# Hats' last steps four slots later, a projection load on another queue, two more steps ahead of a resizing product

## The chip, the cores and the metric

The kernel runs on one core of one Trainium2 chip. The metric is the device time of one execution in microseconds (us). Before the change three runs took 9247.16, 9256.04 and 9267.85 us; the median is 9256.04 us.

A core has five instruction streams that wait for each other by semaphores: TensorE (PE, whose weight loads stand apart as PEld), VectorE (DVE), ScalarE (ACT), GpSimd (POOL) and SyncE (SP). Each runs its own instructions strictly in order. A DMA is issued by an instruction on SP, ACT or POOL; if that instruction has to wait, everything behind it on the same engine waits too. The profile numbers the DMA queues: q1 carries what SP issues, q10 what ACT issues, q0 what POOL issues.

## The reference, cut to what matters

The input is 32 images of 96 x 56 x 56 floats. Layer 0 is an inverted bottleneck: a 1x1 expansion to 576 channels, a depthwise 3x3, a squeeze gate, a 1x1 **projection** back to 96 channels and a residual sum. Layer 1 takes that sum `x` and does this:

```python
mag = jnp.abs(jnp.fft.rfft2(x, norm='ortho'))
fe = mag.mean(1, keepdims=True)                 # summed over channels, then resized to 56 x 56
...
y = x * ca * sa                                 # channel and spatial attention, both from mag and x
magy = jnp.abs(jnp.fft.rfft2(y, norm='ortho')).mean(1, keepdims=True)
freq_e = jax.image.resize(magy, (b, 1, h, w), method='bilinear')
aux = jnp.concatenate([y, coord, freq_e], 1)
offset = _conv(aux, off_w, off_b, (1, 1))       # 9 taps x 2 coordinates for each pixel
gate = jax.nn.sigmoid(_conv(jax.nn.relu(_conv(aux, dg1_w, dg1_b, (1, 1))), dg2_w, dg2_b))
y_base = _conv(y, base_w, base_b, (1, 1))
sampled = _grid_sample_taps(y, px, py)          # bilinear samples of y at pixel + offset
y_def = jnp.einsum('bcthw,oct->bohw', sampled, def_w.reshape(c, c, 9))
z = (1 - gate) * y_base + gate * y_def          # then a normalisation over all images, and relu(zn + x)
```

## The kernel before, in words

Three stages of three different images are worked on at once, and `layers` weaves their instructions together.

- **The bands** (image b). An image is cut into 7 bands of 8 rows. The samples of a band are made without a gather: for each tile of 4 x 4 pixels the bilinear weights over an 8 x 8 block of y are written as a matrix and multiplied with that block on PE (`sample_tiles`, L725), ACT copies the products to `v` (L729), `pack` (L736) copies the last taps of `v` to spare partitions, and `deform` (L744) multiplies `v` with the deformable weights. A band has two halves of 7 tiles.
- **second(b+1)**: `attend`, the projection of layer 0 and both attentions of the next image.
- **first(b+2)**: `hidden`, expansion and depthwise of the image after that.

`second` and `first` are Python generators. Each `yield` ends a step. The bands set the beat: each call of `pump` is a **slot**, a band has 17 of them (one after each of its 14 tiles, three at its end), so an image has 119. In each slot `pump` takes from each generator as many steps as are due, then runs what stands in the list `later` with a slot number that has been reached:

```python
streams[:] = [[second(b + 1), 0, n_second, slot + 3, slot + length - 8],
              [first(b + 2), 0, n_first, slot, slot + length]]
...
due = st[2] * min(1.0, (slot - st[3]) / (st[4] - st[3]))
```

Here `length` is 119 and the count starts at the image's sixth band (`turn` = 5). `n_second` is counted by running `second(0)` once; counting the yields gives 61, and 40 for `n_first`. So step k of `second` comes at slot x = floor(3 + 108 (k - 1) / 61) + 1 of its image, which is used below.

What the change touches:

- **Hats** (`offsets`, L648 to 679). While band n is sampled, the offsets of band n+2 are found: joint convolution (L606, with `hid` L626), offsets copied to `at` (L655) and written to DRAM as `od` (POOL's queue, L659); in the ninth step SP loads them back, repeated over partitions, as `ht` (L671, one buffer only). Six steps later ACT turns distances into hat weights, max(0, 1 - |d|), with two activations in place (L674, L675), and the next step writes them to DRAM as `hd` on ACT's queue (L678). The generator gets one step at the band's start and one after each of the 14 tiles, so the activations stand behind the last tile's copies, ahead of `pack`, and L678 behind `pack`. `weights_load` (SP, L689 and L690) reads `hd` half a band later into `wc` and `wr`, DVE multiplies them (L696), and the half after that uses them on PE.
- **The projection** (`project_loads` L300 to 307, `project` L315 to 337). The depthwise output lies in DRAM (`h2d`, written by ACT's queue, L224). The projection makes 7 rows of each image half at a time, q = 0 to 3. Its input comes in two tiles with one buffer each: `hq0` (units 0 to 3, the first image half) and `hq1` (units 4 to 8). Per q there are four steps: matmuls on `hq0` (L324); the load of `hq0` for q+1; matmuls on `hq1` (L324, L330), ACT's two copies (L334) and the load of `hq1` for q+1; the residual sum and store on POOL (L467, L468).
- **The resizing product** (`resized_spectrum`, L420 to 436). One step sums the magnitudes over channels on DVE (`m2`, named `m_fe` or `m_fy`, L428); the next multiplies the sum with the resizing matrix on PE (L431). It runs twice for each image.
- **The transforms' loads** (`dft_mag`, L362): after the projection the three first groups of `x` are loaded by SP from what POOL stored.

Who orders what: SP's instructions stay exactly in the order in which the program issues them (`manual_schedule`). The other engines' order is chosen by a scheduler when the program is built; `keep_in_program_order` pins one instruction behind everything issued earlier on its engine.

Of the kernel before, what the change touches and what calls it, by code (L numbers as in the profile page):

```python
# [7 lines left out]
FP = mybir.dt.float32  # L8
I32 = mybir.dt.int32
AF = mybir.ActivationFunctionType  # L10
# [23 lines left out]
EW = ER * W  # L34
NBD = H // RB
BW = NBW
TS = 4
NTX = W // TS
# [4 lines left out]
SB = TS + 2 * REACH  # L43
NS = SB * SB
KP = NTAP * TP
# [256 lines left out]
def project_loads(nc, p, h2d, q, half):  # L302

    u0, u1 = ((0, NCH - 1), (NCH - 1, len(UNITS)))[half]
    hq = p["hq"].tile([128, u1 - u0, EW], FP, name=f"hq{half}")
    nc.sync.dma_start(hq, h2d[u0:u1, :, q * EW : (q + 1) * EW].rearrange("u p n -> p u n"))
    return [(UNITS[u][0], hq[:, u - u0]) for u in range(u0, u1)]


# [112 lines left out]
def resized_spectrum(nc, p, mag, name, scale=None):  # L422


    m2 = p["sp"].tile([2 * WX, V], FP, name=f"m_{name}")
    if scale is not None:
        nc.vector.tensor_tensor(mag, mag, scale.unsqueeze(2).to_broadcast([2 * WX, NP, V]), ALU.mult)
    nc.vector.tensor_reduce(m2, mag.rearrange("p q u -> p u q"), AX.X, ALU.add)  # L428
    yield
    pf = p["acc"].tile([128, 512], FP, name="acc")  # L430
    nc.tensor.matmul(pf[:V, : 2 * W], m2, p["w"]["RT2"], start=True, stop=True)  # L431
    rs = p["sp"].tile([V, 2, W], FP, name=name)
    nc.scalar.copy(rs.rearrange("p m w -> p (m w)"), pf[:V, : 2 * W])
    p["resized"] = rs
    yield


def attend(tc, p, b, x, h2d, pooled, x1, given=False):
# [7 lines left out]
    if not given:  # L446
        NQ = HH // ER
        first = project_loads(nc, p, h2d, 0, 0)
        yield from squeeze(nc, p, pooled)
        rows = [first, project_loads(nc, p, h2d, 0, 1)]  # L450
        for _ in range(2):
            yield
        for q in range(NQ):
            at = q, q + NQ
            xrs = [residual_load(nc, p, x, k) for k in at]
            outs = project(nc, p, rows)
            next(outs)
            yield
            if q + 1 < NQ:
                first = project_loads(nc, p, h2d, q + 1, 0)  # L460
            yield
            os = next(outs)
            if q + 1 < NQ:
                rows = [first, project_loads(nc, p, h2d, q + 1, 1)]
            yield
            for k, o, xr in zip(at, os, xrs):
                nc.gpsimd.tensor_tensor(o, o, xr, ALU.add)  # L467
                nc.gpsimd.dma_start(x1[:, k * EW : (k + 1) * EW], o)  # L468
            yield
# [10 lines left out]
    nc.scalar.mul(s3[:, 0], pm[:H, :W], 1.0 / C)  # L480
    yield
    yield from resized_spectrum(nc, p, mag, "fe")
    fe = p["resized"]
    mas = p["sp"].tile([2 * WX, 2, NP], FP, name="mas")
# [82 lines left out]
    yield from dft_mag(nc, p, x1, sa)  # L567
    yield
    yield from resized_spectrum(nc, p, p["magnitude"], "fy", cx)
    fy = p["resized"]  # L570
    pz = p["acc"].tile([128, 512], FP, name="acc")
# [48 lines left out]
def joint_conv(nc, p, yp, j, hid):  # L620


    w = p["w"]
    pa = bank(p)
    conv3(nc, pa[:, :BW], w["joint"], yp, CJ, j)
    nc.scalar.activation(hid, pa[:DMID, :BW], AF.Relu, bias=w["dg1b"][:DMID])  # L626
    yb = p["yb"].tile([C, BW], FP, name="yb")
    yield yb, pa[OFF0 : OFF0 + NOFF, :BW]
    nc.scalar.activation(yb[BC:], pa[OFF0 + QC :, :BW], AF.Identity, bias=w["cv"]("base_b")[BC:])
    pb = bank(p)  # L630
    for k in range(NTAP):
        dy, dx = divmod(k, 3)
        r0 = j * RB + dy + PD - 1
        for i in range(2):
            nc.tensor.matmul(pb[i * BC : (i + 1) * BC, : BW // 2].rearrange("p (h w) -> p h w", h=RB // 2), w["base"][:, k],  # L635
                             yp[:C, r0 + i * RB // 2 : r0 + (i + 1) * RB // 2, dx + PD - 1 : dx + PD - 1 + W],
                             start=(k == 0), stop=(k == NTAP - 1))
    yield
    for i in range(2):
        nc.scalar.activation(yb[:BC, i * BW // 2 : (i + 1) * BW // 2], pb[i * BC : (i + 1) * BC, : BW // 2], AF.Identity,  # L640
                             bias=w["cv"]("base_b")[:BC])
    yield


def offsets(nc, p, yp, j, top, hid, ybs, hds):

    w = p["w"]
    joint = joint_conv(nc, p, yp, j, hid)  # L650
    yb, pa = next(joint)
    ybs.append(yb)
    at = p["off"].tile([NOFF, NTX, 2, TP], FP, name="at")
    for s in range(2):
        nc.vector.tensor_copy(at[:, :, s].rearrange("o t (r c) -> o t r c", r=TS),  # L655
                              pa[:, s * BW // 2 : (s + 1) * BW // 2].rearrange("o (r t c) -> o t r c", r=TS, t=NTX))
    yield
    od = p["dp"].tile([NTX, 2, NOFF, TP], FP, name="od")
    nc.gpsimd.dma_start(od.rearrange("t s o p -> o (t s) p"), at.rearrange("o t s p -> o (t s) p"))  # L659
    yield  # L660
    next(joint)
    yield
    next(joint)
    yield
    next(joint, None)
    nc.vector.tensor_reduce(top, at.rearrange("o t s p -> o (t s p)"), AX.X, ALU.max, apply_absolute_value=True)
    for _ in range(4):
        yield
    ht = p["ht"].tile([SB * NTX, 4, KP], FP, name="ht")
    src = od.rearrange("t s o p -> t (s o p)").unsqueeze(0).to_broadcast([SB, NTX, 4 * KP])  # L670
    nc.sync.dma_start(ht.rearrange("q n k -> q (n k)"), src)  # L671
    for _ in range(6):
        yield
    p["tc"].keep_in_program_order(nc.scalar.activation(ht, ht, AF.Abs, bias=w["blk"]))  # L674
    nc.scalar.activation(ht, ht, AF.Relu, bias=w["one"], scale=-1.0)  # L675
    yield
    hd = p["dp"].tile([4, SB, NTX, KP], FP, name="hd")
    nc.scalar.dma_start(hd.rearrange("x i t n -> (i t) x n"), ht)  # L678
    hds.append(hd)


def weights_load(nc, p, hd, h):
# [237 lines left out]
def padded(nc, p, a, images):  # L920

    cp = p["cp"]
    yps = [cp.tile([CJ, HY, WY], FP, name=f"yp{i}") for i in range(images)]
    for t in yps:
        nc.gpsimd.memset(t, 0.0)
        nc.sync.dma_start(t[C : C + 4, PD : PD + H, PD : PD + W], a["coord"])
        nc.sync.dma_start(t[CA:, PD : PD + H, PD : PD + W], a["place"])
    p["x2"], p["n_x2"] = [cp.tile([2 * H, CG, WX], FP, name=f"x2_{i}") for i in range(3)], 0
    for t in p["x2"]:
        nc.gpsimd.memset(t, 0.0)  # L930
    p["s4"] = [cp.tile([H, 3, WP], FP, name=f"s4_{i}") for i in range(2)]
    for t in p["s4"]:
        nc.gpsimd.memset(t, 0.0)
    return yps
# [8 lines left out]
def layers(tc, a, dp, x1d, zd, stats, far):  # L943
# [6 lines left out]
    nc = tc.nc  # L950
    B = x1d.shape[0]
    with ExitStack() as ctx:
        p = {"tc": tc, "dp": ctx.enter_context(tc.tile_pool(name="l1d", bufs=3, space=DRAM))}
# [3 lines left out]
        yp, = padded(nc, p, a, 1)  # L957
        top = p["cp"].tile([NOFF, NBD + 1], FP, name="top")
# [20 lines left out]
        streams, later = [], []  # L979
        slot = 0  # L980
# [96 lines left out]
        bands = [(b, j) for b in range(B) for j in range(NBD)]  # L1077
        hids, gates, ybs, hds, ready = [], [], [], [], []

        def find(n):  # L1080
            if n % 2 == 0:
                hids.append(p["hid"].tile([2 * NS, BW], FP, name="hid"))
            hid = hids[n // 2][n % 2 * NS : n % 2 * NS + DMID]
            return offsets(nc, p, yp, bands[n][1], top[:, n % NBD : n % NBD + 1], hid, ybs, hds)

        for n in range(2):
            for _ in beside(find(n)):
                pass
# [20 lines left out]
        for n, (b, j) in enumerate(bands):  # L1109
            if j == 0:  # L1110
                st = p["st"].tile([C, NBD, 6], FP, name="st")
            if j == turn:
                drain()
                refill(b + 1, 3 * RB)
                flush()
                start(b + 1, slots)
            more = find(n + 2) if n + 2 < len(bands) else iter(())
            next(more, None)
            for h in range(2):
# [385 lines left out]
```

## Time and profile before

| | |
|---|---|
| three runs, us | 9247.16, 9256.04, 9267.85 |
| the profiled execution, us | 9239.07, of which 9237.3 is the span |
| mean granted PE clock | 0.933 |
| busy PE / PEld / DVE / ACT / POOL | 89% / 56% / 78% / 58% / 27% |
| steady part, 700 to 8925 us | PE busy 7664.74 of 8225 us, DVE 6590.52, ACT 4998.23; PE clock 0.95; DMA engines 0.56 |
| start, 0 to 700 us | PE busy 539.88 us |
| end, 8925 to 9237 us (normalisation) | PE busy 17.22 us, DMA engines 0.91 |

How to read the views. "Busy" is the time in which an engine has an instruction under way. The view of waits names, for each engine, the instruction that sat idle, what ended the wait, the sum in us, how often, and the longest. The timeline lists instructions with their start and length; the bracket is the idle time before the first one and what ended it. The view of stretches gives, for a window of the span, the busy time of each engine, the granted PE clock (1.00 is full speed), the mean busy share of the 16 DMA engines and GB/s. A queue's name with q (SPq, ACTq) is the sequencer that waits and issues DMAs. In the steady part an image takes about 269 us, and the pattern of one image repeats in the next.

### The profile page before, as it was taken

The numbers are of one execution on the slowest core, as the hardware profiler recorded it, in microseconds if no ns is written. First come the engines' busy times: TensorE is split into PE (matmuls) and PEld (weight loads), VectorE is DVE, ScalarE is ACT, GpSimd is POOL, SyncE is SP. The second block draws the span as 40 slices with busy tenths as digits, with TensorE's granted clock in tenths as the row PEclk, the third lists the DMA queues.
The fourth block names the chain that finished last, engine by engine and source line by source line (L and its number), as shares of the span: only waits on it lengthen the run. The fifth ranks groups of instructions, "written<-read, shape, count | busy, mean of one in ns | idle before, by whom it ended". The sixth has DMA issues, their size and how long they took to land. (4 is left out here: it accounts for less than half of the span.)

```text
span 9237.3 us, 138081 instructions
## 1 busy us (share of the span) xinstructions
PE 8221.8 (89%) x52406; PEld 5208.4 (56%) x52406; DVE 7198.1 (78%) x6693; ACT 5369.4 (58%) x10486; POOL 2529.9 (27%) x2611
## 2 busy tenths in 40 slices
PE   5889999999999999899999999999999999999870
PEld 3455565565555556555555655555565655655550
DVE  7587788888888888887888888788888888887333
ACT  2355566666666566665566665566666655666553
POOL 0123233323223322332332223233222323322210
PEclk9889999999999999999999999999999999999985
DMA  2345555555555555555555555555555555554559
GB/s 88 95 137 156 165 166 159 165 150 150 161 163 163 163 164 149 150 157 165 163 157 160 148 153 157 164 167 159 159 152 153 160 166 163 160 160 140 131 181 417
DMA packets 1068764, 1486.54 MB, mean 161 GB/s; under 512 B 590190, under 2 KB 839838, under 8 KB 1055806
## 3 DMA queue, kind: packets, MB, share of 16 engines
q1 hardware_dynamic: 858995, 985.20, 39.2%
q10 hardware_dynamic: 153803, 329.80, 9.8%
q0 software_dynamic: 55296, 162.60, 6.8%
q8 instruction: 421, 6.90, 0.3%
q14 instruction: 249, 2.04, 0.1%
HBM read 1064.29 MB, written 412.65 MB: 160 GB/s over the span
## 5 line engine op out<-in xcount | busy, mean ns | idle before, releaser
L262 DVE SCALAR_TENSOR_TENSOR acch<-hp,w,acch 128x1512 f32<-128x1512 f32 (+1 forms) x2250 | 4397.3, 1954 | 38.2
L606 PE MATMUL mm<-yp,c_jointW 104*128 104x448 f32 x4032 | 1674.2, 567 | 27.7 <-ACT sq L414 19.2
L744 PE MATMUL pd<-v,c_def 128*96 128x224 f32 (+1 forms) x6272 | 1450.9, 378 | 225.2 <-ACT v L736 201.6
L707 POOL COPY ybl<-yp 96x448 f32<-96x448 f32 x896 | 1079.8, 1232 | 1698.5 <-PE mm L711 1697.5
L744 PEld LDWEIGHTS pd<-v,c_def 128*96 128x96 f32 (+1 forms) x6272 | 1046.2, 174 | 524.7 <-ACT v L736 229.2
L606 PEld LDWEIGHTS mm<-yp,c_jointW 104*128 104x128 f32 x4032 | 772.4, 196 | 808.1 <-issue 737.9
L725 PE MATMUL mm<-wc,yt 64*96 64x144 f32 x12544 | 1065.7, 298 | 56.8 <-ACT hp L173 38.0
L169 PE MATMUL mm<-xt,w 96*128 96x392 f32 (+3 forms) x2688 | 1061.2, 529 | 36.4 <-DMA xt<-in_x 33.0
L173 ACT ACTIVATE hp<-mm,sh,inv 128x392 f32<-128x392 f32 (+2 forms) x1216 | 813.2, 673 | 445.4 <-PE mm L169 400.6
L696 DVE TENSOR_TENSOR wc<-wc,wr 128x1008 f32<-128x1008 f32 x448 | 579.5, 1293 | 622.2 <-DMA wr<-hd 614.4
L729 ACT COPY v<-mm 96x288 f32<-96x288 f32 (+1 forms) x2688 | 1001.7, 443 | 100.3 <-PE mm L725 61.3
L725 PEld LDWEIGHTS mm<-wc,yt 64*96 64x96 f32 x12544 | 830.6, 162 | 358.5 <-issue 171.3
L324 PE MATMUL mm<-hq,w3s 128*96 128x392 f32 x2048 | 798.4, 537 | 157.2 <-DMA hq<-h2d 155.8
L635 PE MATMUL mm<-yp,c_base0W 96*64 96x224 f32 x8064 | 828.0, 357 | 0.0
L736 ACT COPY v<-v 32x448 f32<-32x448 f32 x1344 | 755.2, 562 | 29.9
L659 POOL DMA_DIRECT2D od<-at x224 | 186.0, 830 | 1947.6 <-DVE at L655 1386.0
L635 PEld LDWEIGHTS mm<-yp,c_base0W 96*64 96x64 f32 x8064 | 553.2, 135 | 276.2 <-issue 69.3
L713 ACT COPY yt<-mm 128x384 f32<-128x384 f32 (+1 forms) x896 | 350.1, 440 | 519.2 <-PE mm L711 514.5
L324 PEld LDWEIGHTS mm<-hq,w3s 128*96 128x96 f32 x2048 | 340.7, 175 | 513.6 <-issue 323.7
L222 ACT ACTIVATE acch<-acch,sh,inv 128x1568 f32<-128x1568 f32 x288 | 488.6, 1696 | 207.3 <-DVE acch L262 205.0
L626 ACT ACTIVATE hid<-mm,c_dg1b 50x448 f32<-50x448 f32 x224 | 140.7, 628 | 794.7 <-PE mm L606 784.6
L467 POOL TENSOR_TENSOR o<-o,xc 96x392 f32<-96x392 f32 x256 | 366.3, 1431 | 679.3 <-ACT o L334 677.8
(194 smaller groups left out, 9038.8 us busy)
## 6 DMA issues: line engine op xcount, KB each, us to landing
h2d<-acch ACTq DMA_DIRECT2D x288, 784.0 KB
wc<-hd SPq DMA_DIRECT2D x896, 252.0 KB
wr<-hd SPq DMA_DIRECT2D x896, 252.0 KB
hq<-h2d SPq DMA_DIRECT2D x128, 980.0 KB
hq<-h2d SPq DMA_DIRECT2D x128, 784.0 KB
x<-x1d SPq DMA_DIRECT2D x768, 98.0 KB
ht<-od SPq DMA_DIRECT2D x224, 252.0 KB
hd<-ht ACTq DMA_DIRECT2D x224, 252.0 KB
```

Of the source, the lines that this page charges most:

```text
L169: nc.tensor.matmul(pt[p0 : p0 + w1.shape[1], : rows * W], w1, xts[hf][:, r0 * W : (r0 + rows) * W], start=True, stop=True)
L173: nc.scalar.activation(h1[lo:hi, row0 : row0 + rows, 1 : 1 + W], pt[lo:hi, : rows * W].rearrange("p (h w) -> p h w", h=rows), AF.Silu, bia ...
L262: nc.vector.scalar_tensor_tensor(acc[:, lo:hi], win, wk, acc[:, lo:hi], ALU.mult, ALU.add)
L324: nc.tensor.matmul(pts[half][:C, :EW], w3s[:, ch], hq, start=(i == 0), stop=False)
L606: nc.tensor.matmul(view, weights[:, k], yp[:channels, r0 : r0 + RB, dx + PD - 1 : dx + PD - 1 + W], start=(k == 0), stop=(k == NTAP - 1))
L635: nc.tensor.matmul(pb[i * BC : (i + 1) * BC, : BW // 2].rearrange("p (h w) -> p h w", h=RB // 2), w["base"][:, k], yp[:C, r0 + i * RB // 2 ...
L696: p["tc"].keep_in_program_order(nc.vector.tensor_tensor(wc, wc, wr, ALU.mult))
L707: nc.gpsimd.tensor_copy(yb[:, :, s], blocks)
L725: nc.tensor.matmul(pt[k][:C, (t - lo) * KP : (t - lo + 1) * KP], yt[ps, t], s[ps, t * KP : (t + 1) * KP], start=True, stop=True)
L729: nc.scalar.copy(v[:C, :, lo:hi, k].rearrange("c k t p -> c t k p"), pt[k][:C, : (hi - lo) * KP].rearrange("c (t k p) -> c t k p", t=hi - ...
L736: nc.scalar.copy(v[C:, 1 + 2 * i : 3 + 2 * i], v[i * QC : (i + 1) * QC, KA:])
L744: nc.tensor.matmul(out.rearrange("c q (t x) -> c t q x", x=TS), p["w"]["def"][ks, k], v[ks, k].rearrange("c t s (r x) -> c t (s r) x", r=T ...
```

## The change

Three edits. Hats' two activations and the write of `hd` become one function that is put in `later` with the current slot plus four, instead of being the generator's last two steps. The load of `hq0` is issued on ACT's queue, pinned in program order there; `hq1` stays on SP's. Two empty steps are put between the channel sum and the resizing product.

```diff
     hq = p["hq"].tile([128, u1 - u0, EW], FP, name=f"hq{half}")
-    nc.sync.dma_start(hq, h2d[u0:u1, :, q * EW : (q + 1) * EW].rearrange("u p n -> p u n"))
+    src = h2d[u0:u1, :, q * EW : (q + 1) * EW].rearrange("u p n -> p u n")
+    if half:
+        nc.sync.dma_start(hq, src)
+    else:
+        p["tc"].keep_in_program_order(nc.scalar.dma_start(hq, src))
...
     nc.vector.tensor_reduce(m2, mag.rearrange("p q u -> p u q"), AX.X, ALU.add)
     yield
+    yield
+    yield
     pf = p["acc"].tile([128, 512], FP, name="acc")
...
-def offsets(nc, p, yp, j, top, hid, ybs, hds):
+def offsets(nc, p, yp, j, top, hid, ybs, hds, defer):
...
     for _ in range(6):
         yield
-    p["tc"].keep_in_program_order(nc.scalar.activation(ht, ht, AF.Abs, bias=w["blk"]))
-    nc.scalar.activation(ht, ht, AF.Relu, bias=w["one"], scale=-1.0)
-    yield
-    hd = p["dp"].tile([4, SB, NTX, KP], FP, name="hd")
-    nc.scalar.dma_start(hd.rearrange("x i t n -> (i t) x n"), ht)
-    hds.append(hd)
+
+    def hats():
+        p["tc"].keep_in_program_order(nc.scalar.activation(ht, ht, AF.Abs, bias=w["blk"]))
+        nc.scalar.activation(ht, ht, AF.Relu, bias=w["one"], scale=-1.0)
+        hd = p["dp"].tile([4, SB, NTX, KP], FP, name="hd")
+        nc.scalar.dma_start(hd.rearrange("x i t n -> (i t) x n"), ht)
+        hds.append(hd)
+
+    defer(hats)
...
-            return offsets(nc, p, yp, bands[n][1], top[:, n % NBD : n % NBD + 1], hid, ybs, hds)
+            return offsets(nc, p, yp, bands[n][1], top[:, n % NBD : n % NBD + 1], hid, ybs, hds,
+                           lambda hats: later.append((slot + 4, hats)))
```

## The prediction

> **What bounds the kernel now.** I read the page first:
>
> ```profile
> PE 8221.8 (89%) x52406; PEld 5208.4 (56%) x52406; DVE 7198.1 (78%) x6693; ACT 5369.4 (58%) x10486; POOL 2529.9 (27%) x2611
> ```
>
> PE is the bound: the sum of its work sets the time, and only what keeps it idle or slow can be won. Next the steady part in the view of stretches (columns: length, busy of PE, PEld, DVE, ACT, POOL, PE clock, DMA share, GB/s):
>
> ```profile
> 700.00:8925.00 8225.00, 7664.74 (x49732) 4876.09 (x49733) 6590.52 (x5928) 4998.23 (x9880) 2410.76 (x2475) 0.95 0.56 157
> ```
>
> PE is idle for 560 us of it (8225 - 7665), and a clock of 0.95 loses up to 411 us more (0.05 x 8225). Then the waits of PE (sum, times, longest); these four rows hold 461 us, and the change touches all four:
>
> ```profile
> PE pd L744 <- ACT v L736: 201.6, 73, 8.0
> PE mm L324 <- DMA hq<-h2d: 155.8, 31, 9.9
> PE acc L431 <- DVE m_fe L428: 59.9, 30, 2.6
> PE acc L431 <- DVE m_fy L428: 43.8, 32, 11.0
> ```
>
> Last the timeline of one image around each. For the first row, PE and ACT:
>
> ```profile
> 4304.02 0.56 ACT L736 COPY v<-v 32x448 f32<-32x448 f32 x1
> ...
> 4311.76 0.78 ACT L674 ACTIVATE ht<-ht,c_blk 112x576 f32<-112x576 f32 x1 [5.57 <-DMA ht<-od]
> ...
> 4314.69 1.15 ACT L736 COPY v<-v 32x448 f32<-32x448 f32 x2
> ...
> 4315.30 3.30 PE L744 MATMUL pd<-v,c_def 128*96 128x224 f32 x8 [6.74 <-ACT v L736]
> ```
>
> ACT stands for `ht` with two of `pack`'s three copies behind hats, and PE stands for those copies. Followed one by one, 30 of the 73 waits, one an image, are of this kind and hold 177 of the 201.6 us, 5.9 us each. `ht` is late because SP stood until 4294.2 us for the store of the projection's last rows, and issued it at 4301.87. After the stall PE is slow:
>
> ```profile
> 4269.00:4280.00 11.00, 11.00 (x26) 5.23 (x26) 8.02 (x6) 0.68 (x1) 0.51 (x1) 0.82 0.50 169
> 4312.00:4320.00 8.00, 4.70 (x16) 4.03 (x16) 8.00 (x8) 5.34 (x10) 0.00 (x0) 0.50 0.47 108
> 4355.00:4358.00 3.00, 3.00 (x5) 1.33 (x4) 3.00 (x5) 2.96 (x7) 0.00 (x0) 0.50 0.64 261
> ```
>
> The middle row follows this stall: 4.70 us at half clock lose 2.35. The first follows a wait for `hq` that ended at 4268.6 (0.18 x 11 = 2.0), the third a wait of only 1.99 us for `m_fe` (1.5). So a stall costs its idle time plus some 2 us.
>
> The page on "TensorE: Matmul & The Clock Gate" of the Trainium skill (HAM oscillation) warns of idle gaps over about 3.4 us. By that the 1.99 us gap would cost no clock, and part three below would be worth only its idle time, 104 us. The row just shown says otherwise, and I go by the row.
>
> **Part one: hats.** Removed from between the last tile's copies and `pack`: two activations (0.775 and 0.771 us) and one DMA issue (0.33 us). They come back in the third pump after the last tile, behind `pack` and behind what the streams issue in three slots (269 / 119 = 2.3 us each). Nothing is added. ACT now copies `v` at once, so PE's L744 does not wait. What is late next: PE goes on to L387, whose `x` of the fourth group is issued at 4305.75 behind `ht` and `wc`/`wr` in SP's queue, so I let 2.85 us of the 8.25 (5.9 + 2.35) come back as waits for `x` and their slow clock. Gain 30 x 5.4 = 162 us; bounds 0 and 30 x 8.25 = 248.
>
> `hd` comes about 7 us later (three slots). Behind it in SP's order stand `wc`, `wr` and the next `ht`. The cover is large: SP waits for `hd` in 41 places only, and the product on DVE (L696) ends 3 to 16 us before PE's first use in nearly all steady half bands; PE waits for it once in the whole span, 6.0 us. I cost it at 0; if the cover went, the price is 41 x 6.8 = 280 us. In the last eight bands, with no streams, ACT reaches hats before `ht` lands (waits of 0.2 to 1.6 us), so they move only behind 1.7 us of `pack`: 0. At the start both first hats now wait for one flush, and the second `ht`, with one buffer, waits for the first hats. PE already waits 5.98 us for `wc` at 440.9; the first two hats stand at 406.9 and 430.5, so the loss is 0 to 23.6 us; I take 7.
>
> **Part two: `hq0` on ACT's queue.** Now it is queued behind others on SP, and DMA is full:
>
> ```profile
> 4247.91 0.37 SPq L306 DMA_DIRECT2D hq<-h2d  x1
> ...
> 4250.97 0.66 SPq L671 DMA_DIRECT2D ht<-od  x1
> 4253.20 9.08 SPq L306 DMA_DIRECT2D hq<-h2d  x2
> ...
> 4262.00:4269.00 7.00, 1.06 (x3) 0.46 (x3) 4.77 (x3) 3.29 (x5) 4.00 (x6) 0.80 0.98 279
> ```
>
> Ahead of the `hq0` issued at 4253.20 stand `hq1` (980 KB), four `wc`/`wr` (1008 KB) and `ht` (252 KB); it lands at 4268.5, and PE waits from 4262.7. It is always the load for q=3. On ACT it no longer queues behind those. It would stand behind the write of `h2d` (784 KB) if that were issued first: `first` writes unit 0 at slot 27, and step 14, this load, is at floor(3 + 108 x 13 / 61) + 1 = 27. But part three makes 61 steps 65, and step 14 moves to floor(3 + 108 x 13 / 65) + 1 = 25. So it goes ahead and needs some 6 us at half of 270 GB/s, with 10 until PE's use.
>
> The bytes remain, though. With 65 steps the load of `hq1` for q=3 (step 15) is at slot 27, its use (step 19) at 33; before they were 28 and 35, with the next band's joint convolution (18 x 0.38 = 7 us) between. From 4247 on are asked for: `hq1` of q=2 (980 KB), `wc`/`wr` (1008), `ht` (252), `hq0` (784), `h2d` (784), POOL's four rows of 147, and `hq1` of q=3 (980), together 5.4 MB, which at 270 GB/s land at about 4267. PE, not held up, reads `hq0` at some 4261.5, and after 2.6 us of those matmuls and 1.5 of pumps `hq1`, at 4265.6. So I expect a wait of about 2 us there. Of 5.0 idle and 2.0 clock I keep 3.8 (the rest is that new wait and its clock): 31 x 3.8 = 118 us; bounds 0 (it lands no sooner) and 31 x 7 = 217.
>
> The page "DMA: Bandwidth & Descriptors" (Issuing engines are not separate DMA queues) says that issuing from several engines saves only the time to issue. By it this part is worth 0 and the sum below some 90 us less. The 0.98 row agrees that nothing is free; I hold that order, not bandwidth, made this load late.
>
> ACT gets 128 issues of 0.33 us, 42 us in all, in an engine 58% busy: 0. A trigger must wait for PE's last read of `hq0` with all of ACT behind it. That read is one step older, and ACT's copies ahead of it wait for later matmuls anyway: 0, up to the row that SP pays now:
>
> ```profile
> SPq L306 <- PE mm L324: 628.1, 95, 13.3
> ```
>
> SP loses that wait; what stood behind, `ht` and `wc`, comes earlier, costed at 0 since `hq1`'s wait follows.
>
> **Part three: two steps more.** L428 and L431 stand 1 to 2 slots apart, with the square root and the sum between; afterwards 5. Nothing is executed more. The two rows hold 103.7 us idle and about 21 times 1.5 us + some of clock, some 150 us; I keep 130 (bounds 0 and 150). Also, projection and first transform move two to four slots earlier against the bands, so `x` of the transform is asked for before the second half band's loads: this helps part one.
>
> **The sum.** 162 + 118 + 130 = 410. A faster PE meets DVE sooner: in one image DVE is busy 221.35 of 269 us, and 13 us less leave it 35 idle. I take a quarter off: 307, less 7 at the start: 300. The profiled execution took 9239.07 (span 9237.3 and 1.8 around); 9239 - 300 = 8939, and as the median lies 17 us above that execution, I say 8955.
>
> **The rivals.**
> - *The waits only change places* (no full gain): DMA stays at 0.89 to 0.98 in the projection, PE waits for `hq1` and `x` instead, and only part three and a third of part one pay: 130 + 54 - 7 = 177, down to 30: 9080 to 9230. For it: the 0.98. Against: DMA share is only 0.56 on the whole.
> - *All of it goes*: 248 + 217 + 150 = 615, less a fifth: about 8760, range 8750 to 8850. Against: DVE's load.
> - *ACT stands in SP's place* (slower): ACT's trigger for `hq0` waits for PE as SP's does, 6.6 us in 95 places, and `v`'s copies behind it hold up PE. At full reach +628 - 292 (parts one and three) = +336, 9590; it turns the sign from 47% of it, 3.1 us a trigger. For it: ACT issues in order and the load is pinned. Against: ACT mostly waits for the same PE.
> - *It does not do what it says*: hats are still reached before `ht` lands, because ACT has little else in three slots; then part one falls: 0.75 x 248 - 7 = 179, so 9077, at the edge of the first rival.
>
> **How the numbers follow.** Forecast (8850 to 9080) 0.52; waits change places 0.22; all goes 0.09; within 0.2% of 9256, about what a measurement of this kernel can tell from no change, 0.04; slower 0.13. The range 8800 to 9230 leaves out slower, same and the lowest few. Faster 0.83, same 0.04, slower 0.13.
>
> **What would show it.** Part one right: the wait of L744 for L736 falls under 60 us and ACT's wait for `ht`, now 270.2 us in 98 places, under 100. Part two: the L324 wait under 80 us, named for `hq1`; wrong if ACT shows an L306 wait of hundreds of us. Part three: both L431 rows nearly gone. The steady clock should rise to 0.97. Wrong altogether if PE waits for `wc`, or if new PE waits at L387 exceed 100 us.

## The result and the profile after

The change made the kernel slower. The changed kernel ran 9506.53 us (median of 4, 9481.58 to 9514.43), beside it the kernel before 9251.6 (4 runs, 9239.62 to 9267.85): a ratio of 1.0271, 95% interval 1.0249 to 1.0293. 8955 was forecast, with a range of 8800 to 9230.

Line numbers have moved: L324 is now L328, L387 is L391, L414 is L418, L431 is L437, L725 is L734, L729 and L736 are L738 and L745, L744 is L753. First the page and the steady part (columns as before):

```profile
PE 8273.0 (87%) x52406; PEld 5262.1 (55%) x52406; DVE 7155.0 (75%) x6693; ACT 5394.3 (57%) x10501; POOL 2527.2 (27%) x2611
```

```profile
700.00:9187.00 8487.00, 7723.49 (x49653) 4934.63 (x49653) 6548.33 (x5924) 5018.56 (x9884) 2408.14 (x2474) 0.94 0.55 152
```

PE has the same matmuls. It idles 764 us in the steady part (8487 - 7723) where it idled 560, and its clock is 0.94. Its waits (sum, times, longest):

```profile
PE mm L328 <- DMA hq<-h2d: 270.4, 69, 8.6
PE mm L391 <- POOL x L371: 199.6, 65, 5.4
PE mm L734 <- ACT sq L418: 62.1, 17, 6.2
...
PE pd L753 <- ACT v L745: 4.9, 17, 1.0
...
PE acc L437 <- DVE m_fy L432: 4.0, 2, 2.6
...
PE acc L437 <- DVE m_fe L432: 3.1, 2, 2.7
```

Three of the four rows that the change aimed at are gone: `pack`'s copies (201.6 to 4.9) and both sums (103.7 to 7.1). The fourth, `hq`, grew from 155.8 to 270.4. Two kinds that were small before are large: PE waits for POOL's weighing of `x` in the second transform, and for ACT's squares (62.1 at the sampling, 55.4 at the expansion; 2.9 and 1.4 before). The weighing's row before:

```profile
PE mm L387 <- POOL x L367: 18.0, 24, 3.4
```

To compare kernels of different speed I use an account per image, worked out from the trace: PE's gaps over 0.15 us between the third and the 31st write of `sad` (28 images), and for each stretch at a lower clock PE's busy time in it times what the clock lacks, put down to the longest gap that overlaps it or ended less than 8 us before it. All in us per image; in the rows by cause the idle time and the half-clock time are added.

| | before | hats alone | steps alone | hats and steps | queue alone | changed |
|---|---|---|---|---|---|---|
| one image | 269.45 | 267.98 | 270.38 | 272.02 | 274.15 | 279.17 |
| PE idle | 18.02 | 14.65 | 16.64 | 19.02 | 20.24 | 25.30 |
| lost at half clock | 9.78 | 11.37 | 12.41 | 11.74 | 11.20 | 12.37 |
| what remains | 241.65 | 241.96 | 241.34 | 241.27 | 242.72 | 241.51 |
| deform for `v` | 9.97 | 0.40 | 6.13 | 2.28 | 10.93 | 2.33 |
| projection for `hq` | 7.28 | 7.28 | 4.18 | 5.47 | 9.09 | 11.49 |
| products for the sums | 4.46 | 4.57 | 0 | 0 | 4.35 | 0 |
| transform for the weighing | 0.28 | 0.24 | 8.53 | 8.64 | 0.18 | 8.78 |
| sampling and expansion for ACT's squares | 0.17 | 0.57 | 0.10 | 6.18 | 0 | 6.63 |

What remains is the same within 1.5 us in all six, so nearly all of the difference is waits and the slow clock behind them. Each column comes from one profiled execution, up to 24 us off its kernel's median, which is 0.8 us an image; smaller differences tell nothing. The changed image is 9.72 us longer, 272 us over the 28; the two spans differ by 262.

### The profile page after: what moved, and what is told of

The parts are those of the page before. It is cut to its first block, busy times and chain, and to the rows that moved or that the text cites. A ratio compares the mean times of both kernels' runs of the same rounds, so it can differ in the third digit from the quotient of the medians.

```text
span 9498.9 us, 138255 instructions
## 1 busy us (share of the span) xinstructions
PE 8273.0 (87%) x52406; PEld 5262.1 (55%) x52406; DVE 7155.0 (75%) x6693; ACT 5394.3 (57%) x10501; POOL 2527.2 (27%) x2611
## 5 line engine op out<-in xcount | busy, mean ns | idle before, releaser
L262 DVE SCALAR_TENSOR_TENSOR acch<-hp,w,acch 128x1512 f32<-128x1512 f32 (+1 forms) x2250 | 4313.3, 1917 | 36.0 <-ACT hp L173 3.4
L716 POOL COPY ybl<-yp 96x448 f32<-96x448 f32 x896 | 1133.2, 1292 | 2081.8 <-PE mm L720 2081.7
L612 PE MATMUL mm<-yp,c_jointW 104*128 104x448 f32 x4032 | 1618.7, 553 | 36.0 <-DMA yp<-fqd 35.8
L753 PE MATMUL pd<-v,c_def 128*96 128x224 f32 (+1 forms) x6272 | 1497.9, 388 | 55.6 <-ACT v L738 50.1
L753 PEld LDWEIGHTS pd<-v,c_def 128*96 128x96 f32 (+1 forms) x6272 | 1085.5, 180 | 410.8 <-issue 123.4
L734 PE MATMUL mm<-wc,yt 64*96 64x144 f32 x12544 | 1091.1, 298 | 121.5 <-ACT sq L418 62.1
L169 PE MATMUL mm<-xt,w 96*128 96x392 f32 (+3 forms) x2688 | 1100.2, 540 | 93.1 <-ACT sq L418 55.4
L328 PE MATMUL mm<-hq,w3s 128*96 128x392 f32 x2048 | 816.8, 547 | 300.8 <-DMA hq<-h2d 270.4
L738 ACT COPY v<-mm 96x288 f32<-96x288 f32 (+1 forms) x2688 | 1002.2, 443 | 129.7 <-PE mm L734 92.1
L734 PEld LDWEIGHTS mm<-wc,yt 64*96 64x96 f32 x12544 | 830.1, 161 | 440.8 <-issue 180.2
L705 DVE TENSOR_TENSOR wc<-wc,wr 128x1008 f32<-128x1008 f32 x448 | 558.0, 1246 | 469.4 <-DMA wr<-hd 455.4
L745 ACT COPY v<-v 32x448 f32<-32x448 f32 x1344 | 755.3, 562 | 29.3
L328 PEld LDWEIGHTS mm<-hq,w3s 128*96 128x96 f32 x2048 | 353.4, 179 | 685.3 <-issue 628.0
L391 PE MATMUL mm<-c_FU,x 112*128 112x116 f32 x3072 | 462.0, 298 | 214.1 <-POOL x L371 199.6
L391 PEld LDWEIGHTS mm<-c_FU,x 112*128 112x128 f32 x3072 | 425.6, 209 | 307.1 <-POOL x L371 224.3
```

Source lines behind the costliest of these rows:

```text
L169: nc.tensor.matmul(pt[p0 : p0 + w1.shape[1], : rows * W], w1, xts[hf][:, r0 * W : (r0 + rows) * W], start=True, stop=True)
L262: nc.vector.scalar_tensor_tensor(acc[:, lo:hi], win, wk, acc[:, lo:hi], ALU.mult, ALU.add)
L328: nc.tensor.matmul(pts[half][:C, :EW], w3s[:, ch], hq, start=(i == 0), stop=False)
L391: nc.tensor.matmul(pt[:, i * 4 * V : (i + 1) * 4 * V], x2s[g][:, 2 * i : 2 * i + 2, :].rearrange("h c w -> h (c w)"), w["FU"], start=True, ...
L612: nc.tensor.matmul(view, weights[:, k], yp[:channels, r0 : r0 + RB, dx + PD - 1 : dx + PD - 1 + W], start=(k == 0), stop=(k == NTAP - 1))
L716: nc.gpsimd.tensor_copy(yb[:, :, s], blocks)
```

## The experiments

Each time is a median, beside runs of the kernel before on the same chip; ratios are to those.

**One part at a time, and all but one.** The edits are the hunks of the change.

> Only hats' last steps move four slots; the load of hq0 and the 61 steps stay as before. Theory Q (the load on ACT's queue is the loss: SP issued it far ahead of its use, ACT issues it where ACT stands): this part alone is faster, 9090 to 9180 us, the wait of L744 for pack falls from 201.6 us to under 60. Theory S (61 to 65 steps moves the projection and the second transform against the bands): the same 9090 to 9180. Theory H (hd comes later, SP stands for it 1277 us instead of 560 and all loads behind it are late): this part alone is slower, 9350 or more, with SP's wait for hd over 1000 us.

Measured: 9200.73, ratio 0.9941 (0.992 to 0.9963). The deform's wait went, as expected, but a third of the gain arrived, short of the expected 9180; theory H, which had this part slower, falls. PE's waits:

```profile
PE mm L387 <- DMA x<-x1d: 54.9, 19, 10.6
...
PE mm L387 <- DVE sq L373: 30.6, 13, 3.7
...
PE pd L747 <- ACT v L732: 16.4, 37, 0.9
```

Before, L387 waited 15.6 us for `x`, and no row for VectorE's `sq` stood there. PE, not held at the deform, comes sooner to the first transform and to the sampling, and waits there for the loads of `x`, for VectorE's sums (`sq`; by the source they read a PSUM bank, which PE fills again later) and for ACT: `hp` 46.1 us against 38.0, `yb` 25.7 against 3.3.

> Only the load of hq0 moves to ACT's queue. Theory Q: slower, 9400 to 9550 us, with PE's wait for hq at 250 us or more, most of it released by loads that ACT issued. Theory S: within 1% of 9252 or a little faster, since the alignment is the old one; PE's wait for hq at most 155 us. Theory H: the same as S.

Measured: 9368.4, ratio 1.012 (1.0096 to 1.0144): theory Q's direction, but less than its 9400 and its wait of 250 us. ScalarE's load is what PE now waits for. The view of the line L310 (who waited, us, times):

```profile
  PE mm L328: 193.6, 62
```

ACT also stands ahead of this load, 260 us in the whole run, 172 of them at q = 1, whose load waits for PE's last read for q = 0. In one image ACT's copies end at 4292.32 and the issue comes 7.2 us later:

```profile
4290.61 1.71 ACT L740 COPY v<-v 32x448 f32<-32x448 f32 x3
4299.54 0.38 ACTq L310 DMA_DIRECT2D hq<-h2d  x1
```

> Only the two empty steps are added at each resizing product, so second has 65 steps. Theory Q: faster by the 104 us of the two L431 rows and their slow clock, 9100 to 9180 us. Theory S: slower, 9350 to 9500 us, with PE's new wait for POOL's weighing of x (199.6 us after) present here too. Theory H: 9100 to 9200 us.

Measured: 9231.25, ratio 0.9974 (0.9957 to 0.9991). That is neither Q's time nor S's, though the wait that S named is there. Both sums' waits went, the weighing's came:

```profile
PE mm L387 <- POOL x L367: 188.0, 65, 5.4
```

> Hats and steps as changed, the load of hq0 back on SP's queue. Theory Q: faster than before, about 9000 us (162 and 130 us of the forecast). Theory S: still slower than before, 9300 to 9500 us. Theory H: still slower, 9300 us or more, with SP's wait for hd over 1000 us.

Measured: 9284.69, ratio 1.0032 (1.0018 to 1.0045). That lies between Q's 9000 and S's 9300. Hats and steps, each a small gain alone, are a small loss together: the steps alone had already taken 3.8 of the deform's 10 us, so hats had less to give, and ACT's squares cost 6.2 us an image in this pair and next to nothing in either alone.

**Why the queue costs.** The load of q = 0 in one image of the changed kernel, ACT's timeline and then PE's:

```profile
4314.90 0.38 ACTq L310 DMA_DIRECT2D hq<-h2d  x1
```

```profile
4328.16 2.24 PE L328 MATMUL mm<-hq,w3s 128*96 128x392 f32 x3 [7.70 <-DMA hq<-h2d]
```

ACT issued it 5.6 us ahead of the moment when PE wanted it (4328.16 - 7.70 = 4320.46), and PE's wait for it ended 13.3 us after the issue. SyncE's timeline shows what it shared the DMA engines with, `hq1` and `ht`, and between them four `wc` and `wr`:

```profile
4312.07 0.39 SPq L308 DMA_DIRECT2D hq<-h2d  x1
...
4315.19 0.66 SPq L677 DMA_DIRECT2D ht<-od  x1
```

In the kernel before SyncE issued this load at 4190.02 (one line with the next load, issued at 4203.71), and the first read came at 4216.9, 27 us later:

```profile
4190.02 14.08 SPq L306 DMA_DIRECT2D hq<-h2d  x2
```

SyncE in this kernel only issues and waits, so it can be far ahead of PE; ACT issues where it stands between its copies. The lead from issue to PE's first want (median over 28 images) and the mean gap ahead of PE's first matmul on the load:

| first-half load | q = 0: lead, wait, us | q = 3: lead, wait, us |
|---|---|---|
| before (SyncE) | 26.9, 0 | 9.5, 5.02 |
| queue alone | 9.2, 3.41 | 10.1, 2.86 |
| changed | 6.0, 6.64 | 8.7, 1.03 |
| changed, q = 0 back on SyncE | 19.8, 0 | 8.7, 1.26 |
| before, only q = 1 to 3 on ScalarE | 26.9, 0 | 10.1, 2.63 |
| steps alone (SyncE) | 21.4, 0 | 10.9, 0.88 |
| hats and steps (SyncE) | 19.6, 0 | 10.8, 1.13 |

So the queue takes 18 us of lead at q = 0 when it is alone (26.9 to 9.2) and 14 us with hats and steps (19.6 to 6.0). What it was to give, the wait at q = 3, the steps alone had mostly taken already (5.02 to 0.88); on top of hats and steps it gives 0.1 there. A short lead by itself does no harm: in the changed kernel the load of q = 1 has 5.0 us and PE never waits for it. No other DMA is issued within 4 us of that one, and the DMA engines are busy to 0.51 in the 5 us behind its issue; behind that of q = 0 they are to 0.94.

The test puts one load of four back:

```diff
-    if half:
+    if half or q == 0:
         nc.sync.dma_start(hq, src)
```

> The changed kernel, but the projection's first-half load of q = 0 goes back to SyncE's queue; those of q = 1 to 7 stay on ScalarE's. Theory L (a load on ScalarE's queue starts only where ScalarE stands, SyncE ran ahead of the program; it hurts at q = 0, where TensorE waits 5.8 us an image in the changed kernel and not at all before): the q = 0 wait goes and with it the half-clock stretch behind it, about 7 us an image over 31 images, 9507 to some 9290 or below. Rival T (the queue shift costs by the extra load on ScalarE or by slower transfers, whichever q it is): one load of eight moved back gives one eighth, under 30 us, 9480 or above. Rival D (the loads of q >= 1 are what delays ScalarE): no change within 20 us, and a wait of the same size at another q.

(There are four first-half loads an image, q = 0 to 3; where this and later expectations write q up to 7, read 3, and their q = 6 is q = 3. By that rival T gives a quarter of what the queue cost, 222 / 4, 9450.) Measured: 9237.79, ratio 0.9976 (0.9966 to 0.9985), 269 us below the changed kernel. Theory L holds, and by more than expected; T and D fall. The wait for `hq` in this kernel:

```profile
PE mm L328 <- DMA hq<-h2d: 89.1, 47, 7.6
```

The same edit on the kernel before, without hats and steps:

> The kernel before, with the projection's first-half loads of q = 1 to 7 on ScalarE's queue and that of q = 0 left on SyncE's. Theory L: of part two of the change alone (9368) the 3.1 us wait at q = 0 goes with its half-clock stretch, some 4.5 us an image, 31 x 4.5 = 140 less, 9230; and what the change was meant to do stays, 2.2 us of the wait at q = 6, which would bring it to some 9190 if no other wait grew. So 9180 to 9240, below before's 9256. Rival T (the load on ScalarE costs by its wait in ScalarE's queue): 9300 or above, with TensorE's wait for v's copies still 0.8 us an image above before's.

Measured: 9195.12, ratio 0.9924 (0.99 to 0.9948). This is what the edit could give: 59 us. The wait at q = 3 halves, and no other wait grows by more than 10 us (`pack`'s, from 201.6 to 211.0). Theory L again, and T falls:

```profile
PE mm L328 <- DMA hq<-h2d: 86.1, 34, 8.2
```

**Why the steps give nothing.** The timeline of POOL around the weighing, steps alone:

```profile
4138.47 2.69 POOL L367 TENSOR_TENSOR x<-x,sa 112x448 f32<-112x448 f32 x1
4145.82 1.41 POOL L1052 DMA_DIRECT2D zd<-z  x1 [4.66 <-DVE z L787]
4147.25 1.14 POOL L367 TENSOR_TENSOR x<-x,sa 112x448 f32<-112x448 f32 x1
```

And PE in the same kernel:

```profile
4148.44 0.77 PE L387 MATMUL mm<-c_FU,x 112*128 112x116 f32 x2 [5.40 <-POOL x L367]
```

POOL stands 4.66 us for VectorE's last step on a band (`z`) in order to store it, with the last weighing behind the store, and PE stands for that weighing. Before, the store stood ahead of weighings too, but sooner: counted from the write of `sad` in the image at the same place, the store was issued at 18.9 us, the last weighing began at 21.4 and PE's last group at 23.3; with the steps the store is issued at 24.4, the weighing begins at 25.8, and PE wanted it at 21.6. In the account of the steps alone the weighing loses 8.3 us an image and two waits for ACT (`gate` and `t`) 4.6, while the sums gain 4.5, the deform 3.8 and `hq` 3.1; so little is left either way.

Two steps behind the product instead of ahead of it keep every other step's slot and add no distance:

```diff
     nc.vector.tensor_reduce(m2, mag.rearrange("p q u -> p u q"), AX.X, ALU.add)
     yield
-    yield
-    yield
...
     p["resized"] = rs
     yield
+    yield
+    yield
```

> The kernel before, with the two empty steps of each spectrum behind its resizing product instead of ahead of it: as many steps in all, so every later step falls into the same slot as in the steps alone, but no more distance between a spectrum's sum and its product. Theory A (the steps act through two things: the distance removes TensorE's waits for the sums, 4.5 us an image with their half-clock stretches, and the changed slots bring the wait for the weighing, 8.5 us an image): both the waits for the sums stay and the wait for the weighing comes, about 9231 + 31 x 4.5 = 9370, above 9320 at the least. Rival B (the distance itself makes what comes after it late): no wait for the weighing, time within 60 us of before.

Measured: 9257.52, ratio 1.0011 (0.999 to 1.0032). The time is far below A's 9320. Half of theory A holds: the wait for the weighing comes with the slots alone. The other half holds for one sum and falls for the other: without any distance in the program the wait for `m_fe` goes (59.9 before, 3.8 here), that for `m_fy` mostly stays (43.8 before).

```profile
PE mm L387 <- POOL x L367: 182.9, 65, 5.4
...
PE acc L431 <- DVE m_fy L428: 34.4, 32, 4.3
...
PE acc L431 <- DVE m_fe L428: 3.8, 3, 2.6
```

From the start of the sum of `m_fe` to its product it is a median of 5.2 us here, 6.8 with the steps and 2.7 before; for `m_fy` 2.6 here, 6.4 with the steps and 2.6 before. So the slots alone part the first pair, and the second needs the distance. The reverse edit gives distance without slots, one step ahead of the first product and one less behind it:

```diff
+    if name == "fe":
+        yield
...
     p["resized"] = rs
-    yield
+    if name != "fe":
+        yield
```

> The kernel before, with the first spectrum's resizing product one step later and the empty step behind that product taken away: one step more of distance, as many steps in all as before, every other step in its old slot. If the distance is worth what the prediction took it for, TensorE's wait for the sum (2.0 us an image and 1.7 us of half clock behind it) goes and no wait for the weighing comes: 31 x 3.7 = 113 less than 9256, some 9145. Rival G (a wait taken from TensorE is given back in part at the next engine, as with the hats, 57 of 162): 9190 to 9230, with new waits of 1 to 3 us an image elsewhere. Rival N (one step is too little or the product only moves into another stall): the wait for the sum stays, 9240 or above.

Measured: 9257.85, ratio 1.0002 (0.9989 to 1.0016): rival N. In PE's order of 52,406 matmuls 4 stand elsewhere than before, and the product stands right behind its sum as it did:

```profile
PE acc L433 <- DVE m_fe L428: 59.5, 30, 2.6
```

So one empty step put no distance between these two instructions, whose engine the scheduler orders. Two put some between `m_fy` and its product, and the four shifted the slots of all that follows. The next two runs go at the store ahead of the weighing. The first moves it two slots:

```diff
-            later.append((slot + 7, lambda: store(b, j, z)))
+            later.append((slot + 9, lambda: store(b, j, z)))
```

> The hats four slots later and the two steps, all projection loads on SyncE, and the store of a finished band (zd) two slots later than it is (nine after the join's half instead of seven). Theory P (GpSimd works in program order; with two steps more per spectrum the store, which waits for VectorE's last step on the band, stands ahead of a weighing of the second transform, and TensorE waits for that weighing): TensorE's wait for the weighing falls from 6.3 us an image to under 1.5, its half-clock stretch of 2.4 us with it, 9285 to some 9050, faster than before by 2%. Rival W (the weighing is late because VectorE and GpSimd slow one another, its rows read 2.3 to 2.7 us instead of 1.1): the wait stays above 4 us an image and the time within 60 us of 9285. Rival V (the wait goes and another takes its place): wait under 1.5 us an image, time above 9200.

Measured: 9286.7, ratio 1.003 (1.0016 to 1.0043), as without it. The run tells nothing about P, since POOL's 2611 instructions in the trace stand in the same order as without the edit. So does the second run with this edit:

> The changed kernel with both mends, the q = 0 load back on SyncE and the store of a band two slots later. If theories L and P hold and the two add: 9507 less 217 less 235 to 265, some 9030 to 9060, near the kernel with all loads on SyncE and the later store; what it is below that kernel is what loads of q >= 1 on ScalarE's queue are worth. If either mend only moves the wait, 9200 or above.

Measured: 9232.25, ratio 0.9969 (0.9952 to 0.9986), within 6 us of the kernel with the q = 0 load alone put back. The second edit pins the store:

```diff
-            nc.gpsimd.dma_start(zd[b][:, j * BW : (j + 1) * BW], z)
+            tc.keep_in_program_order(nc.gpsimd.dma_start(zd[b][:, j * BW : (j + 1) * BW], z))
...
-            later.append((slot + 7, lambda: store(b, j, z)))
+            later.append((slot + 13, lambda: store(b, j, z)))
```

> The hats four slots later and the two steps, all projection loads on SyncE, and the store of a band 13 slots after its join instead of 7 and pinned in program order on GpSimd, so that it stands behind the second transform's last weighing and no longer ahead of it (the store two slots later left GpSimd's order as it was, so that run told nothing). Theory P (the store, which waits for VectorE's last step on the band, holds the last weighing up): of TensorE's wait for the weighing the 5.4 us part goes, 0.9 to 1.5 us an image stay, the half-clock stretch of 2.4 us goes with it; 31 x 7.3 = some 225 us less than 9285, 9060. Rival W (weighing slow by itself): wait above 5 us an image, 9285 within 50 us. Rival V (PE is bound there by something else that is late too, VectorE's work on the band or the transform's own chain): the wait goes, another of more than half its size comes, 9150 to 9285.

Measured: 9223.78, ratio 0.9971 (0.9955 to 0.9986), 61 us below hats and steps without this edit. PE's waits:

```profile
PE mm L608 <- ACT sq L414: 81.1, 25, 5.2
...
PE mm L387 <- POOL x L367: 59.8, 46, 2.6
```

The mechanism of P is shown: the weighing's wait falls from 195.0 to 59.8. But rival V has the time: with its half-clock share the wait loses 6.3 us an image, and the joint convolution (L608) gains one of 4.8 for ACT's squares.

**Why the hats gave a third.** Two slots instead of four (`slot + 2`):

> The hats two slots later instead of four, nothing else. Theory G (four slots removed 9.5 us an image of TensorE's waits for v's copies, and TensorE, no longer held there, meets VectorE's sums, the x loads and ScalarE's hp instead, 8 us an image): with two slots the wait for v's copies is as small, below 2 us an image, and the same new waits stand, 9190 to 9220. Rival O (the new waits come from where the hats now stand in ScalarE's order, or from hd being later): other waits than with four slots, and a time that differs by more than 30 us either way, 9170 or below if the later place is what cost.

Measured: 9168.75, ratio 0.9911 (0.9888 to 0.9933). The deform's wait is as small (0.9 us an image with its half clock), and VectorE's sums, `x` and `hp` stand among PE's waits again: theory G. But it is 32 us faster than four slots (9156.57 to 9186.6 against 9187.97 to 9210.43), so part of what was given back belongs to the place, as rival O has it. In the account that is half-clock time, 9.28 us an image against 11.37, not idle time, 15.31 against 14.65; why the place does this is not shown.

```profile
PE mm L387 <- DVE sq L373: 68.6, 31, 4.3
```

**What is worth keeping.** Three versions without the added steps, the q = 0 load left on SyncE:

> The hats four slots later and the loads of q = 1 to 7 on ScalarE's queue, that of q = 0 on SyncE's, no added steps. If the parts add: the hats alone 9201, less what the loads of q = 1 to 7 are worth alone (some 20 to 70), 9130 to 9180, faster than both kernels. If they don't add, since TensorE freed of one wait meets the next (VectorE's sums, ScalarE's hp): 9200 or above.

Measured: 9139.08, ratio 0.9874 (0.9849 to 0.99). 57 and 59 alone, 115 together: these two parts add.

> The hats four slots later, the first-half loads of a later q on ScalarE's queue with that of q = 0 left on SyncE's, and the first spectrum's resizing product one step later at the same number of steps. That without the product's move ran 9139. If the wait for the sum goes in full, 31 x 3.9 = 120 less, 9020; if a half is given back, some 9080; if all of it is, 9139. Likeliest 9080, and faster than both kernels either way.

Measured: 9152.94, ratio 0.9892 (0.9873 to 0.9911). As the product alone, its move gives nothing.

> The hats two slots later and the first-half loads of a later q on ScalarE's queue, that of q = 0 on SyncE's; no added steps. If the parts add as they did with four slots (57 and 59 alone, 115 together): 9169 less 59, some 9110. If TensorE's waits for the projection's load are already partly gone with two slots (2.9 us an image of 5.0 left), the loads are worth half: some 9140. In both cases faster than the kernel before; below 9139 only in the first.

Measured: 9117.7, ratio 0.9838 (0.9822 to 0.9854), the fastest version found, 140 us below the kernel before and 389 below the change. Its two largest waits:

```profile
PE mm L328 <- DMA hq<-h2d: 84.4, 33, 7.4
PE mm L391 <- DVE sq L377: 64.6, 33, 6.4
```

## Why the prediction was wrong

The forecast had the wrong sign. By its own steps:

- **What bounds the kernel** held: in every run PE's work without gaps and slow clock is 241 to 243 us an image. So did the price of a stall, some 2 us: the changed image has 6.2 gaps over 1.5 us and 5.0 half-clock stretches that lose 12.37 us, the one before 3.7 and 3.7 that lose 9.78. The steady clock, expected at 0.97, is 0.94.
- **Part one** (162): right in mechanism, wrong in size. Alone it gave 57. Its two tests came true: L744 for `pack` at 4.9 us in the changed kernel (under 60), ACT's wait for `ht` 5.4 (under 100). The term that was mis-sized is the 2.85 us let come back of 8.25. Of 9.6 us an image that left the deform, 8.1 came back elsewhere, most of it at `x`, VectorE's sums, `yb`, and `hp` with its half clock. For this part the rival "the waits only change places" had the size, 54. Taking the hats two slots later instead leaves 0.9 us at the deform and gives 91 us: a part of the give-back is the place. That `hd`'s delay costs PE next to nothing held (two waits for its product, 7.2 and 7.5 us, where there was one of 6.0), though SyncE's waits for it rose from 560.3 to 1276.9 us.
- **Part two** (118): this step failed, and it turned the sign; the row that was to fall under 80 us stands at 270.4. The step looked at the load of q = 3 alone. That one did come sooner, but for half of the 118: 59 us when only q = 1 to 3 move, and next to nothing beside the steps, which shorten the same wait from 5.02 to 0.88 us an image; this the sum counted twice. But "ACT gets 128 issues of 0.33 us, 42 us in all, in an engine 58% busy: 0" took an issue for the time that it occupies, not for the place where it stands. The load of q = 0 lost 18 us of a lead of 26.9, and 14 of 19.6 with hats and steps. With hats and steps present the queue cost 222 us (9285 to 9507); with q = 0 back on SyncE the same kernel is at 9238. The sentence "So it goes ahead", of the write of `h2d`, was about a load that a few us of lead helped, and the one that needed it was overlooked. The rival on the slower side (ACT stands in SP's place) named the right part, and its mechanism is not what slowed the changed kernel: there ACT stands ahead of that load for 12 us in the whole run, and PE stands for the data. In the queue alone it does stand, 260 us in all; the deform's wait for `v` is 0.96 us an image longer there than before, of 4.7 that the queue alone costs, and whether the standing makes it longer was not tested.
- **Part three** (130): failed too, though its test came true (both rows at 7.1 us) and the mark of a wrong prediction, new waits of L387 over 100 us, came with it (199.6). "L428 and L431 stand 1 to 2 slots apart" and "afterwards 5" priced the steps by the distance alone. One step of distance moved 4 of PE's matmuls and no wait; the wait for `m_fe`, 3.7 of the 4.5 us an image, goes with the slots alone, since 65 steps fall into other slots than 61, and only that for `m_fy` needed the distance. The same shift put the store's wait in front of the weighing at PE's cost, 8.3 us an image, a term that the sum does not have. I had counted the shift only where it helped (step 14 and the loads of `x`).
- **The sum.** The three were added and cut by a quarter. Measured alone they are -57, +111 and -26, which adds to +28; together they are +255. Of the 227 between, 110 is parts one and three (-83 added, +27 as a pair: both remove the same deform wait, and ACT's squares come) and 111 is the queue on top of the pair (222 instead of 111: the lead at q = 0 is 6.0 us instead of 9.2, the gap 6.64 instead of 3.41, and at q = 3 nothing was left to gain). Why ACT's squares are late only in the pair was not tried and stays open.
- **The page "DMA: Bandwidth & Descriptors" of the Trainium skill** (Issuing engines are not separate DMA queues) would have made part two 0. As changed it cost 111 alone, with q = 0 left on SyncE it gained 59: the engines are shared, as the 13.3 us for 784 KB beside SyncE's loads show, but who issues decides when, and the section prices the issue alone.

## What to carry to other kernels

Before a DMA moves to another engine's queue, read for every instance of it how far ahead of its use it is issued now; here SyncE, which only issues, was 27 us ahead and ACT 6 to 9, and the instance that never waited was the one that lost. Where a kernel is woven from steps by a count, an added step shifts every later one, for better and worse; and where a scheduler orders the engines, a move in the program is a move only once the trace's order shows it. Take the parts of a change singly and in pairs: the waits that two parts remove can be the same one.

## What the runs showed of the hardware

A gap as short as 1.5 us, with smaller ones of 0.36 and 0.74 us near it, was followed by ten us at half clock. The hats alone, PE's timeline and then the stretches around it (columns as before: the clock is the third number from the end):

```profile
4166.51 0.48 PE L728 MATMUL mm<-wc,yt 64*96 64x144 f32 x2 [0.36 <-ACT yb L640]
4168.50 1.06 PE L728 MATMUL mm<-wc,yt 64*96 64x144 f32 x6 [1.51 <-ACT hp L173]
4170.31 0.57 PE L431 MATMUL acc<-c_RT,m_fy 128*29 128x112 f32 x2 [0.74 <-DMA wr<-hd]
```

```profile
4169.00:4178.90 9.90, 9.15 (x40) 6.67 (x38) 9.87 (x10) 6.04 (x14) 1.05 (x2) 0.50 0.55 193
4180.00:4190.00 10.00, 9.60 (x55) 5.95 (x52) 9.96 (x8) 4.53 (x9) 5.22 (x3) 1.00 0.82 147
```

PE's waits for `hp`, of which this is one, cost 4.2 us of slow clock an image in that kernel with only 1.5 us of idle time.

How often a gap is followed by half clock depends on its length. In the six kernels of the table, among the gaps that began at full clock, half clock began in the gap or within 4 us behind it after 165 of 799 gaps under 1 us, 91 of 195 of 1 to 1.5 us, 185 of 269 of 1.5 to 2 us, 120 of 164 of 2 to 3 us and 323 of 327 longer ones. So the sum of the idle time does not price the slow clock: the hats alone have less idle time than the kernel before (14.65 us an image against 18.02) and more half-clock loss (11.37 against 9.78). Here one has to count the gaps, by length.
